# A fused attention and FFN kernel: attention blocks in another order on every engine, and the rows' turn one job later

## The chip, the cores and the metric

The kernel runs on one core of a Trainium2 chip. The metric is the time of one execution in device microseconds (us), and the median of several runs is compared.

## The reference

The input is one sequence of 2048 rows of 1024 numbers, in 32-bit floats. The reference is a block of a transformer with a norm before and after each half:

```python
x = x + _layernorm(attn(_layernorm(x), Wqkv, bqkv, Wo, bo))
x = x + _layernorm(ffn(_layernorm(x), W_gate, W_up, W_down))

# attn: one head of width 256
qkv = x @ Wqkv + bqkv                      # q, k, v: 2048 x 256 each
attn = softmax(q @ k.T / 16)               # 2048 x 2048
return (attn @ v) @ Wo + bo                # 2048 x 1024
# ffn, F = 2752
return (silu(x @ W_gate.T) * (x @ W_up.T)) @ W_down.T
```

## The kernel before, in words

**Precision.** A 32-bit product is made of three faster ones. Each operand is split into a high part (a copy by ScalarE, ACT, in a rounded format) and a low part (what is left, a subtraction by VectorE, DVE). `mm3` issues high times high, high times low and low times high. So every operand that reaches TensorE (PE) costs ACT one pass and DVE one pass.

**Stages.** First the queries, keys and values are made from the transposed input (to about 150 us). Then attention runs over 16 blocks of 128 queries, `i` from 0 to 15 (to about 400 us). Then comes the FFN in two halves of 1024 rows (`s` is 0 or 1), each with ten pairs of weight columns (`gate_up`) and a product with the down weights (`run_down`).

**One attention block.** While block `i` multiplies its probabilities with the values (`attend(i)`), the softmax of block `i+1` is prepared. In the ten blocks of `SPREAD` (2 to 11) the probabilities are turned with the help of DMAs:

- `scores(i+1, j)`, for four groups `j` of 512 keys: six matmuls and one reduce for the maximum on DVE (L266). `largest` joins the four (L465, L466).
- `exponentials(i+1, ...)`: four ACT passes into `p_s` (L476). After the second and the fourth, ACT's queue issues a store of one half to `pt_d` (L478), in pieces that go to other partitions.
- `collect(i)`: SP's queue loads the two halves of `pt_d` into `wr[0]` and `wr[1]` (L445). `turn_half` transposes each within 32 x 32 squares on DVE (L453), `high_half` (ACT, L457) and `low_half` (DVE, L461) split it.
- `turn_o(i-1)`: PE transposes the output of the block before (L524), ACT and DVE split it (L530, L531). `proj(i-1)` multiplies it with `Wo`, and DVE scales it and adds the bias (L541).
- `attend(i)`: 16 matmuls of 512 and 16 of 256 columns, in four quarters that need high half 0, low half 0, high half 1 and low half 1. ACT copies the sum (L516) and DVE adds the other part (L517).

**Queries.** The queries of the next four blocks come from `q_d` by `q_load` and are split by `q_split` (L435, L436). Blocks 4 to 7 use `qs[1]`, so its split must be done before block 3 computes the scores of block 4.

**Rows.** For the first `EARLY` = 8 blocks the rows that follow are done at once. `out_stats(t)` gives the norm of the projected row block (ACT, L555). `residual(t)` adds it to the row block of `x` (DVE, L559) and stores the sum in `x1_d` (L560). `rows_stats` (ACT, L566, and GpSimd, POOL) and `rows_norm` (ACT, L572) norm it. `spread(t)` stores it from ACT's queue to `xn_d` in another layout (L680), `gather(t)` loads it back on SP's queue (L683), `xpose(t)` transposes it on DVE (L687) and stores it in `xT_d` (L689), from where the FFN takes it. Each of these transfers moves 512 KB, as do the halves of `pt_d` and the load of `x` (L1295). Row blocks use three pairs of tiles in turn (`pair`), which lie in `f4` and `f2p`.

**Late rows.** Row blocks 8 to 15 store their projection in `at_d` (L543) and are finished during the ten pairs of the first FFN half. `gate_up` has four places where it takes one job from a list: after its first two products, after four, after eight and after ten. Before, the jobs of pair `p` are `between(p)` (the gather of the row block before), `ahead(p)` (its transpose, then the loads of the next, then `down_weights(p-1)`) and `behind(p)` (`load_down(p)`, then the norms of the next in `late_residual`, and its spread). The fourth place is used in the last pair alone.

**What sets the order.** The framework orders the instructions of each engine at compile time by a simulation. Instructions handed to `pin` (`tc.keep_in_program_order`) keep the order of the program among themselves on their engine. Engines and the queues that issue DMAs (SP's, ACT's) work in order, so an instruction that waits holds all that stand behind it. Before, the score matmuls and most of ACT's and DVE's work of a block are pinned, and the DMAs are not. Matmuls of a block are in this order: scores 0, 1 and 2, `turn_o`, scores 3, `proj`, `attend`.

Of the kernel before, what the change touches and what calls it, by code (L numbers as in the profile page):

```python
# [34 lines left out]
def block_kernel(ctx, tc, x, xt, wqk, wqk_t, wv, bqk, bv, wo, bo, wgu, wlast, wd, out):  # L35
# [390 lines left out]
    def o_of(i):  # L426

        return o_s[i % 2] if i < NT - 1 else xe[:, 0:D]
# [4 lines left out]
    def q_split(g, pin=lambda i: i):  # L433
        q = qs[g % 2]
        pin(nc.scalar.copy(q[:, :, 0, :], qraw))  # L435
        nc.vector.tensor_tensor(q[:, :, 1, :], qraw, f32(q[:, :, 0, :]), ALU.subtract)  # L436
# [6 lines left out]
    def collect(i):  # L443
        for h in range(2):
            nc.sync.dma_start(wr[h], pt_d[i][h])  # L445
# [53 lines left out]
    def attend(i, pin=lambda i: i):  # L499
# [3 lines left out]
        if i == NT - 1:  # L503
# [4 lines left out]
            nc.scalar.copy(o, b[:, :D])  # L508
# [7 lines left out]
        nc.scalar.copy(o, b[:, :D])  # L516
        nc.vector.tensor_tensor(o, b[:, D:], o, ALU.add)  # L517
# [16 lines left out]
    def proj(i, pin=lambda i: i):  # L534
# [7 lines left out]
        if i >= EARLY:  # L542
            nc.sync.dma_start(at_d[i], a)  # L543
# [14 lines left out]
    def residual(t, a, xt, r, pin):  # L558
        pin(nc.vector.scalar_tensor_tensor(xt, a, r, xt, ALU.mult, ALU.add))  # L559
        nc.sync.dma_start(x1_d[t].rearrange("(g s) c -> s g c", g=4), xt)  # L560
# [10 lines left out]
    def rows_norm(a, xt, r, m):  # L571
        nc.scalar.activation(a, xt, AF.Identity, bias=m, scale=r)  # L572
# [105 lines left out]
    def spread(t, a):  # L678

        nc.scalar.dma_start(by_quarter(xn_d[t]), a.rearrange("p (i c) -> p i c", i=4))  # L680

    def gather(t, b):
        nc.sync.dma_start(b, xn_d[t])  # L683

    def xpose(t, a, b):
# [3 lines left out]
        nc.sync.dma_start(d.rearrange("(j p) t -> p j t", p=P), a.rearrange("p (j t) -> p j t", j=8))  # L689
# [597 lines left out]
    sts = {}  # L1287
    for i in range(NT):
# [3 lines left out]
        if 4 <= i < EARLY + 4:  # L1292
            xpose(i - 4, *pair[(i - 4) % 3])
        if 4 <= i < EARLY + 1:
            nc.sync.dma_start(pair[(i - 1) % 3][1], x[(i - 1) * P : i * P, :])  # L1295
        if i == EARLY + 3:
            first_load(0, *room[0])
        if i in SPREAD:
            collect(i)
            scores(i + 1, 0, pin, pin)  # L1300
            scores(i + 1, 1, pin, pin)
            turn_half(i, 0)
            scores(i + 1, 2, pin, pin)
            turn_o(i - 1, pin, pin)
            high_half(i, 0)
            scores(i + 1, 3, pin, pin)
            largest(i + 1, pin)
            turn_half(i, 1)
            exponentials(i + 1, (0, 1), pin)
            high_half(i, 1)  # L1310
            exponentials(i + 1, (2, 3), pin)
            low_half(i, 0)
            proj(i - 1, pin)
            low_half(i, 1)
            denominator(i + 1, pin)
# [17 lines left out]

        if i < 2:
            wo_split(i)
        if i == 0:
            center_bo()
        if i == 1:
            q_load(1)
        if i == 2:  # L1340
            q_split(1, pin)
        if i % TB == 0 and TB <= i < NT - TB:
            q_split(i // TB + 1, pin)
        if 2 <= i < EARLY + 2:
            residual(i - 2, *pair[(i - 2) % 3], sts[i - 2], pin)
        if i < 3:
            nc.sync.dma_start(pair[i][1], x[i * P : (i + 1) * P, :])
        if i == NT - 1:
            for f in order[2:5]:
                f.use()  # L1350
            for f, r in zip(order[6:8], (wr[1], f4[1])):
                f.load(r)
        if i in SPREAD:
            attend(i, pin)
        else:
            if i > 0:
                turn_o(i - 1)
            attend(i)
            if i > 0:
                proj(i - 1)  # L1360
        if 2 <= i < EARLY + 2:
            of_rows = rows_stats(i - 2, *pair[(i - 2) % 3])
# [150 lines left out]
```

## Time and profile before

| What | Value |
|---|---|
| median of 3 runs (lowest, highest) | 1643.91 us (1643.29, 1647.49) |
| the profiled execution | 1645.07 us, of which the span of its instructions is 1643.3 us |
| PE busy | 1620.4 us, 99% of the span |
| DVE busy | 1117.9 us, 68% |
| ACT busy | 730.9 us, 44% |
| POOL busy | 113.5 us, 7% |
| data moved by DMA | 321.33 MB, 196 GB/s on the mean |
| matmul of 128x128 with 128x512 | 386 to 391 ns each, issued about every 0.23 us |

A busy time is the sum of an engine's instructions. Matmuls overlap (the next one is issued while one drains), so PE can be busy and still not issue at its full rate. A wait in the profile says who waited, and on whose instruction or transfer. The span is cut into stretches where a stage has its own limit: the ten spread blocks run from 176 to 331 us, the pairs of the first FFN half with late rows from about 550 to 800 us.

### The profile page before, as it was taken

How to read it: one execution, taken by the hardware profiler on the slowest of the kernel's cores; microseconds unless marked ns; L12 is line 12 of the kernel's file. 1: busy time of each engine (PE TensorE's matmuls, PEld its weight loads, DVE VectorE, ACT ScalarE, POOL GpSimd, SP SyncE). 2: the span in 40 equal slices, each digit the busy share in tenths (PEclk: the TensorE clock that was granted, in tenths of full speed). 3: DMA queues.
4: the chain of work that ended last, by engine and by line, in shares of the span. 5: the costliest groups of instructions: out<-in, count | busy, mean ns of one | idle time of the engine just before them, and what ended most of it. 6: DMA issues, size and time to landing. Idle time of an engine off the chain costs nothing.

```text
span 1643.3 us, 20534 instructions
## 1 busy us (share of the span) xinstructions
PE 1620.4 (99%) x7416; PEld 1343.8 (82%) x7416; DVE 1117.9 (68%) x1612; ACT 730.9 (44%) x1072; POOL 113.5 (7%) x176
## 2 busy tenths in 40 slices
PE   9999999999999999999999999999999999999998
PEld 8888777787888888888888888888888888888887
DVE  6656788778677777777577458855666655555458
ACT  5664565436444334443465344433333333354342
POOL 3120011000011111120000001100000000000001
PEclk9999999999999999999999999999999999999999
DMA  9451599856657777677477657632222233676653
GB/s 318 161 186 57 182 327 317 303 165 231 224 168 243 239 247 240 231 238 264 149 256 247 195 182 234 203 104 96 96 97 97 103 103 121 243 259 195 192 188 122
DMA packets 161622, 321.33 MB, mean 196 GB/s; under 512 B 15216, under 2 KB 50672, under 8 KB 161520
## 3 DMA queue, kind: packets, MB, share of 16 engines
q1 hardware_dynamic: 141360, 299.18, 54.7%
q10 hardware_dynamic: 20160, 20.84, 3.8%
q8 instruction: 58, 0.95, 0.2%
q14 instruction: 44, 0.36, 0.1%
HBM read 217.19 MB, written 102.78 MB: 195 GB/s over the span
## 4 chain that ended last, share of the span: by engine, by line
PE 75%; DMA 9%; DVE 9%; issue 3%; ACT 2%; POOL 2%; ACTq 0%; SPq 0%; DVEq 0%; POOLq 0%
PE bank L952 59%; DMA xn_d<-f 4%; PE bank L129 3%; PE bank L130 3%; PE bank L131 3%; DMA f<-xn_d 2%; DVE a L113 2%; PE bank L247 1%; PE bank L513 1%; PE bank L515 1%; ACT p_s L476 1%; POOL small L124 1%; DVE small L119 1%; PE bank L248 1%; DVE f L966 1%
## 5 line engine op out<-in xcount | busy, mean ns | idle before, releaser
L952 PE MATMUL bank<-a 128*128 128x512 f32 (+1 forms) x960 | 226.4, 386 | 0.0
L952 PE MATMUL bank<-xb,a 128*128 128x512 f32 x912 | 212.7, 389 | 0.1
L952 PEld LDWEIGHTS bank<-a 128*128 128x128 f32 x960 | 179.1, 188 | 36.5
L952 PEld LDWEIGHTS bank<-xb,a 128*128 128x128 f32 x912 | 170.8, 188 | 35.8 <-DVE a L113 0.5
L112 ACT CAST a<-f2p 128x1024 fp32r<-128x1024 f32 (+2 forms) x123 | 107.2, 871 | 140.6 <-PE bank L952 86.6
L113 DVE TENSOR_TENSOR a<-f2p,a 128x1024 fp32r<-128x1024 f32 (+2 forms) x123 | 122.5, 996 | 44.0 <-ACT a L112 37.0
L952 PE MATMUL bank<-kx,a 128*128 128x512 f32 x612 | 145.2, 389 | 0.0
L952 PEld LDWEIGHTS bank<-kx,a 128*128 128x128 f32 x612 | 114.9, 188 | 23.9
L113 DVE TENSOR_TENSOR a<-f,a 128x1024 fp32r<-128x1024 f32 (+1 forms) x70 | 80.0, 1143 | 64.0 <-ACT a L112 62.0
L952 PE MATMUL bank<-wvo 128*128 128x512 f32 (+1 forms) x498 | 120.9, 386 | 0.0
L952 PEld LDWEIGHTS bank<-wvo 128*128 128x128 f32 x498 | 93.0, 188 | 18.9
L952 PE MATMUL bank<-a,a 128*128 128x512 f32 x420 | 100.3, 391 | 2.5 <-ACT p_s L1014 1.2
L112 ACT CAST a<-f 128x1024 fp32r<-128x1024 f32 (+1 forms) x70 | 57.7, 824 | 98.7 <-PE bank L952 92.7
L952 PE MATMUL bank<-kx,wvo 128*128 128x512 f32 x420 | 99.3, 389 | 0.0
L952 PEld LDWEIGHTS bank<-a,a 128*128 128x128 f32 x420 | 78.4, 188 | 21.2 <-ACT p_s L1014 2.6
L952 PEld LDWEIGHTS bank<-kx,wvo 128*128 128x128 f32 x420 | 78.8, 188 | 16.4
L113 DVE TENSOR_TENSOR wvo<-f,wvo 128x1024 fp32r<-128x1024 f32 (+1 forms) x47 | 54.7, 1164 | 53.3 <-ACT wvo L112 53.3
L966 DVE TENSOR_TENSOR xi<-bank,xi 128x512 f32<-128x512 f32 (+1 forms) x90 | 60.9, 682 | 41.2 <-PE bank L952 34.7
L952 PE MATMUL bank<-a1b,wvo 128*128 128x512 f32 x360 | 86.8, 389 | 0.0
L966 DVE TENSOR_TENSOR p_s<-bank,p_s 128x512 f32<-128x512 f32 x80 | 53.9, 682 | 39.9 <-PE bank L952 36.0
L952 PEld LDWEIGHTS bank<-a1b,wvo 128*128 128x128 f32 x360 | 67.6, 188 | 14.0
L952 PE MATMUL bank<-kx 128*128 128x512 f32 (+1 forms) x339 | 78.5, 387 | 0.0
(366 smaller groups left out, 2982.4 us busy)
## 6 DMA issues: line engine op xcount, KB each, us to landing
f2p<-wgu SPq DMA_DIRECT2D x41, 512.0 KB, 5.5
f<-x SPq DMA_DIRECT2D x28, 512.0 KB, 5.8
f<-wgu SPq DMA_DIRECT2D x22, 512.0 KB, 3.5
wr<-wgu SPq DMA_DIRECT2D x21, 512.0 KB, 5.0
hd_S<-xi SPq DMA_DIRECT2D x42, 256.0 KB, 4.4
pt_d<-p_s ACTq DMA_DIRECT2D x20, 512.0 KB, 4.7
wr<-pt_d SPq DMA_DIRECT2D x20, 512.0 KB, 4.4
f<-wd SPq DMA_DIRECT2D x20, 512.0 KB, 4.3
```

The costliest lines, as they stand in the source:

```text
L112: nc.scalar.copy(hi, src)
L113: (lo_engine or nc.vector).tensor_tensor(lo, src, f32(hi), ALU.subtract)
L119: b = nc.vector.bn_stats(s[:, 6 * i : 6 * i + 6], h)
L124: nc.gpsimd.tensor_tensor(s[:, 15:16], s[:, 14:15], mhalf, ALU.pow)
L129: pin(nc.tensor.matmul(o, w[0], m[0], start=first, stop=False))
L130: pin(nc.tensor.matmul(o, w[0], m[1], start=False, stop=False))
L131: return pin(nc.tensor.matmul(o, w[1], m[0], start=False, stop=last))
L247: pin(nc.tensor.matmul(b, xg[:, c, 0, cols], wv_s[:, c, :, :].rearrange("p a f -> p (a f)"), start=(c == 0), stop=False))
L248: pin(nc.tensor.matmul(b[:, D:], xg[:, c, 1, cols], wv_s[:, c, 0, :], start=False, stop=(c == 7)))
L476: pin(nc.scalar.activation(o, b, AF.Exp, bias=s[:, 5:6], scale=1.0 / 16.0, accum_out=s[:, 8 + j : 9 + j]))
L952: one = nc.tensor.matmul(o, w[i], m[j], start=first and n == 0, stop=last and n == 2, skip_group_check=chained)
L966: nc.vector.tensor_tensor(o, a, b, op)
```

## The change

**The attention blocks.** A spread block is now a function of its own, `block(i)`, and all its instructions on all engines and queues are pinned. Against before:

- `turn_o(i-1)` stands behind the first scores instead of the third.
- The rows of block `i-2` are no longer done at the end of block `i` and on into the next. `rows_in` (residual and store) stands at the start of block `i`, `rows_squares` behind `turn_o`, `rows_out` (norm and spread) before the first high half. In block 2 alone the three stand at the end, before `out_stats`.
- At a block's end stand, in this order, `out_stats(i-1)`, the gather of row block `i-2`, the transpose and store of row block `i-3`, the load of `x`, the collect of the next block's first half, the denominator, the split of queries and `attend(i)`. The second half is collected at the next block's start.
- `q_split` does one half at a time, in two blocks (both halves in block 2).
- In block 9 the transpose of row block 6 writes to `xe` and not to its pair's tile, which is `f4[0]`.
- The output of the last block goes to the end of `p_s` instead of `xe`, and its copy is pinned before the splits of three FFN operands.

**The late rows.** `xpose` of the row block before and the loads of the next move from `ahead` to `behind`. `late_residual` and `spread` move from `behind` to a fourth job, `rows`.

```diff
     def o_of(i):
-        return o_s[i % 2] if i < NT - 1 else xe[:, 0:D]
+        return o_s[i % 2] if i < NT - 1 else p_s[:, T - D :]
...
-    def q_split(g, pin=lambda i: i):
+    def q_split(g, d):
         q = qs[g % 2]
-        pin(nc.scalar.copy(q[:, :, 0, :], qraw))
-        nc.vector.tensor_tensor(q[:, :, 1, :], qraw, f32(q[:, :, 0, :]), ALU.subtract)
+        pin(nc.scalar.copy(q[:, d, 0, :], qraw[:, d]))
+        pin(nc.vector.tensor_tensor(q[:, d, 1, :], qraw[:, d], f32(q[:, d, 0, :]), ALU.subtract))
...
-    def collect(i):
-        for h in range(2):
-            nc.sync.dma_start(wr[h], pt_d[i][h])
+    def collect(i, h):
+        pin(nc.sync.dma_start(wr[h], pt_d[i][h]))
...
+    def load_x(t):
+        pin(nc.sync.dma_start(pair[t % 3][1], x[t * P : (t + 1) * P, :]))
+
+    def rows_in(t):
+        if 0 <= t < EARLY:
+            residual(t, *pair[t % 3], sts[t], pin)
+
+    def rows_squares(t):
+        if 0 <= t < EARLY:
+            of_rows[t] = rows_stats(t, *pair[t % 3])
+
+    def rows_out(t):
+        if 0 <= t < EARLY:
+            rows_norm(*pair[t % 3], *of_rows[t])
+            spread(t, pair[t % 3][0], pin)
+
+    def block(i):
+        first = i == SPREAD[0]
+        if not first:
+            rows_in(i - 2)
+        collect(i, 1)
+        scores(i + 1, 0, pin, pin)
+        turn_o(i - 1, pin, pin)
+        if not first:
+            rows_squares(i - 2)
+        scores(i + 1, 1, pin, pin)
+        scores(i + 1, 2, pin, pin)
+        turn_half(i, 0)
+        if not first:
+            rows_out(i - 2)
+        high_half(i, 0)
+        scores(i + 1, 3, pin, pin)
+        largest(i + 1, pin)
+        turn_half(i, 1)
+        exponentials(i + 1, (0, 1), pin)
+        high_half(i, 1)
+        exponentials(i + 1, (2, 3), pin)
+        low_half(i, 0)
+        proj(i - 1, pin)
+        low_half(i, 1)
+        if first:
+            rows_in(i - 2)
+            rows_squares(i - 2)
+            rows_out(i - 2)
+        if i - 1 < EARLY:
+            sts[i - 1] = out_stats(i - 1, pair[(i - 1) % 3][0])
+        if i - 2 < EARLY:
+            gather(i - 2, pair[(i - 2) % 3][1], pin)
+        if 0 <= i - 3 < EARLY:
+            a, b = pair[(i - 3) % 3]
+            xpose(i - 3, xe if i - 1 == EARLY else a, b, pin)
+            if i < EARLY:
+                load_x(i)
+        if i + 1 in SPREAD:
+            collect(i + 1, 0)
+        denominator(i + 1, pin)
+        if i == 2:
+            q_split(1, 0)
+            q_split(1, 1)
+        elif i % TB < 2:
+            q_split(i // TB + 1, i % TB)
+        attend(i, pin)
...
     def ahead(p):
...
-        if late(p - 1):
-            a, b = rooms(p - 1)
-            xpose(late(p - 1), a, b)
-        if late(p):
-            a, b = rooms(p)
-            nc.sync.dma_start(a, at_d[late(p)])
-            nc.sync.dma_start(b, x[late(p) * P : (late(p) + 1) * P, :])
         down_weights(p - 1)
...
             load_down(p)
+        if late(p - 1):
+            xpose(late(p - 1), *rooms(p - 1))
+        if late(p):
+            a, b = rooms(p)
+            nc.sync.dma_start(a, at_d[late(p)])
+            nc.sync.dma_start(b, x[late(p) * P : (late(p) + 1) * P, :])
+
+    def rows(p):
         if late(p):
             a, b = rooms(p)
             late_residual(late(p), a, b)
...
-            jobs = [] if s else [lambda: between(p), lambda: ahead(p), lambda: behind(p)]
+            jobs = [] if s else [lambda: between(p), lambda: ahead(p), lambda: behind(p), lambda: rows(p)]
             if s == 0 and p == NPAIR - 1:
-                jobs.append(lambda: down_weights(NPAIR - 1))
+                jobs[-1] = lambda: down_weights(NPAIR - 1)
```

The stores and loads of the other row functions (`residual`, `spread`, `gather`, `proj`) and the copies of `attend` get a `pin` of their own.

## The prediction

> **What bounds the kernel now.** I read the page, busy time stretch by stretch, the waits of PE, then the timelines of the queues in the attention blocks.
>
> ```profile
> PE 1620.4 (99%) x7416; PEld 1343.8 (82%) x7416; DVE 1117.9 (68%) x1612; ACT 730.9 (44%) x1072; POOL 113.5 (7%) x176
> DMA  9451599856657777677477657632222233676653
> ```
>
> TensorE (PE) sets the end nearly everywhere; where the DMA digits stand at 9 (the sixth and seventh slices, 205 to 288 us) lie the attention blocks.
>
> ```profile
> 190.16:204.75 14.59, 14.30 (x72) 11.76 (x71) 12.01 (x18) 9.07 (x17) 1.87 (x6) 1.00 0.86 293
> 204.75:218.94 14.19, 14.19 (x72) 11.77 (x71) 12.19 (x19) 10.03 (x18) 1.88 (x6) 1.00 0.95 315
> 249.37:265.37 16.00, 14.32 (x72) 11.77 (x71) 11.93 (x18) 9.07 (x17) 1.68 (x5) 1.00 0.99 330
> 295.66:314.51 18.85, 15.93 (x72) 12.90 (x71) 11.21 (x18) 8.04 (x15) 0.93 (x3) 0.91 0.89 307
> ```
>
> Blocks 3, 4, 7 and 10 (length, busy PE, PEld, DVE, ACT, POOL, clock, DMA share): the same 72 matmuls take 14.19 to 18.85 us. Blocks 2 to 10 last 138.5 us (176.0 to 314.51); nine of 14.05 would be 126.5. So 12.0 us are there to win, 1.7 of it a clock of 0.91 over 18.85 us after a PE idle of 2.9 us.
>
> ```profile
> PE bank L129 <- DVE oTs L531: 6.2, 6, 2.9
> PE bank L524 <- ACT xe L508: 2.5, 1, 2.5
> PE bank L515 <- DVE a L461: 1.8, 2, 1.4
> ```
>
> PE waits for output's transposes (L531), for the last block's output (L508), and for the low half (L461). Behind these stand transfers:
>
> ```profile
> 223.98 7.47 DMA xT_d<-f
> 231.55 1.41 DVE f L541 x2
> ...
> 265.34 4.11 DMA wr<-pt_d
> 269.48 1.25 DVE wr L453
> ...
> 293.46 6.39 DMA at_d<-f
> 299.94 1.25 DVE f L687
> ```
>
> The chain: a row's transposed store holds the projection's L541, the collect of turned probabilities holds L453, the store of `at_d` holds the row transpose L687.
>
> ```profile
> 222.87 0.32 SPq L445 DMA_DIRECT2D wr<-pt_d  x1
> 223.28 0.65 SPq L560 DMA_DIRECT2D x_d<-f2p  x1
> 223.98 0.58 SPq L689 DMA_DIRECT2D xT_d<-f  x1
> 224.62 1.50 SPq L1295 DMA_DIRECT2D f<-x  x1
> ```
>
> SP's queue now: the collects go ahead of the row's store and x load. Landings come one after another: the third of these lands at 231.45 (above), with ACT's `xn_d` store issued between, so the last of four lands 8.58 us after the first issue; a collect alone takes 4.11: (8.58-4.11)/3 = 1.49 us for each further 512 KB. A row block moves nine of them, 13.4 us of a 14.05 us block.
>
> **Part 1, transposes of output behind the first scores.** They move from 6 matmuls before the projection to 18 (12 x 0.2275 = 2.7 us earlier). They need the block before's output: its ACT copy and DVE add end about 1.05 us into the block, the first six scores issue until 1.37. So 0 where DVE is free. The 6.2 us of waits go unless something else holds the blocks.
>
> **Part 2, rows.** Row work runs at a block's start, its transpose at the end. So L541 no longer meets the store (2.7 us of DVE idle), and row 6's transpose writes `xe`, away from `at_d`'s store (3.25 us). But SP's pinned order is now: gather, xT store (needs the transpose, last on DVE), x load, and only then the next block's first collect. This closes a loop. Its DVE part, from a block without waits:
>
> ```profile
> 318.07 1.23 DVE L453 STREAM_TRANSPOSE wr<-wr 128x1024 f32<-128x1024 f32 x1
> ...
> 326.13 0.15 DVE L482 TENSOR_REDUCE ys<-ys 128x1 f32<-128x4 f32 x1
> ```
>
> 8.06 us from the first turn to the end of the low halves; less one reduce (0.60), L531 (0.34) and a wait (0.23), which now come before it, plus the row transpose 1.25: 8.14. The second collect queues behind the first and the x1 store, so it lands 2 x 1.49 = 2.98 later, while DVE asks for it 2.1 later: +0.9. Then SP (0.1), then xT store, load and collect: the store alone 4.2 (the shortest of `xT_d`), two more 2.98: 7.2. The loop is 8.14+0.9+0.1+7.2 = 16.3 us, over PE's 14.05. Without the x load (from block 8 on) it is 14.8. Blocks 4 to 10 follow five loops of 16.3 and two of 14.8 = 111.1; the last queries' load gets between once, +1.5; before they took 314.51-204.75 = 109.8. So +2.8 in place of the gain; block 11 +0.4. Bounds: 14.05 for all seven, -11.4; with 1 us more queueing a block, +10.
>
> The Trainium skill (DMA: Bandwidth & Descriptors, Anatomy of one DMA) fits another issue path with 2.0 us plus bytes/436 GB/s, 1.2 us for 512 KB. By it three transfers take 5.6 us and the loops 14.7 and 14.05; the blocks would lose 8 us of their 109.8. The rows above have 1.49 and 4.1 to 4.2, so I keep those.
>
> **Part 3, the first block.** In block 2, row 0's work and out_stats(1) come before the split of the next queries (L435) on ACT, and block 3's first scores need that split.
>
> ```profile
> 187.76 1.05 ACT L435 CAST qb<-f 128x1024 fp32r<-128x1024 f32 x1 [0.46 <-ACT p_s L476]
> 191.30 1.16 ACT L566 ACTIVATE f<-f,small 128x1024 f32<-128x1024 f32 x1 [0.57 <-DVE f L559]
> 193.76 1.25 ACT L572 ACTIVATE f<-f,small 128x1024 f32<-128x1024 f32 x1 [0.17 <-POOL small L568]
> 195.03 0.37 ACTq L680 DMA_DIRECT2D xn_d<-f  x1
> ```
>
> Now the split runs at 187.76, before. After: low halves end at 187.6, L559 1.28, L566 at 188.9, L572 2.46 later at 191.4, the issue until 193.0, out_stats 1.14, the halves of the split at 194.2 and 194.7, DVE until 196.1. PE wanted it at 190.16: it idles 4.7 us at first and a little within. Gather 0 goes out at 196.5 (row 0's store issued 192.6, 3.9 to land), block 3's first collect behind it lands 4.2+1.49 later, 202.2; PE ends that block 9.1 after (two turns, reduce, largest, the wait of 0.9 and the first low half 5.3, then attend's last three quarters 3.7): 211.4 against 204.75, +6.6. Bounds: +4.7 (the idle alone) and +8.3 with a clock loss of 1.7 as in block 10.
>
> The Trainium skill (TensorE: Matmul & The Clock Gate, What's actually happening) halves the clock after some 3.4 us of idling, by a free-running window; the trace has it after 2.9 us and not after 2.5 (L524). By either, this pause slows PE for a while. Block 3 waits for its collect anyway, so I add nothing.
>
> **Part 4, rows' turn one job later in the first FFN half.**
>
> ```profile
> 603.68 1.25 DVE L687 STREAM_TRANSPOSE f<-f 128x1024 f32<-128x1024 f32 x1 [7.36 <-DMA f<-xn_d]
> ```
>
> DVE stands 7.4 us a pair at L687 for the gather, and PE loses little: 2.5 us idle in 560 to 800 in six gaps, and each restart costs 0.16 more (a matmul lasts 0.39 us, the next one issues 0.23 after it): 3.5. With the transpose one job (24 matmuls, 5.5 us) later and the statistics too, DVE should reach L687 when the gather has landed: -3.3. Moved past on SP: two loads, one store, one gather that waits for its store (5 us of SP). If a weight load is late behind it, it costs instead: bounds -3.5 and +4 (half a us a pair, as PE loses now).
>
> **Part 5, the end.** Output of the last block goes to `p_s`, so L508 (2.5 us of PE idle at 399.2) needn't wait for L747. But the split of `qb` ends at 402.3 on DVE and the next matmuls need it: 0 (bounds -2.6 and +1). Splitting q in halves: 0.1 a time, hidden on ACT (44% busy).
>
> **Sum.** +6.6 +2.8 +0.4 -3.3 = +6.5. The profiled execution took 1645.07 us (span 1643.3 and 1.8 around it), 1.2 above the median of 1643.91; I add to the median: 1650.4.
>
> **Rivals.** (a) Faster: transfers keep up. Decides: if the last of the three lands within 14.05-9.14 = 4.9 us of the store's issue, PE sets blocks 4 to 10: -11.4, the pause in block 2 alone +4.9, FFN -3.3: -9.8, 1634.1. For it: the shortest landing on `pt_d` is 3.0 us; against: DMA shares of 0.95 to 0.99. (b) Between: store 4.2 and 1.3 a transfer, no second wait: loops 15.0 and 14.05, 103.1 us, -6.7; +6.1 for block 2, -3.3: -3.9, 1640.0. (c) As forecast, but SP's gather holds FFN's weights: +4 in place of -3.3: 1657.7.
>
> **Numbers.** Forecast 0.53, (a) 0.15, (b) 0.20, (c) 0.12. What a measurement can tell from no change is 0.3%, 4.9 us: under 1639.0 and over 1648.8. Of the forecast 0.45 lies over, 0.08 within; (b) 0.15 within, 0.05 under; (a) under; (c) over. Faster 0.20, same 0.23, slower 0.57. Range 1640 to 1659: it leaves out (a) and the far end.
>
> **What would show it.** After: PE idle of 4 to 5 us at the start of block 3 for `qb` (L435/436), with a clock under 1; L453 waiting for `wr<-pt_d` in most blocks and blocks near 16 us; L531 gone from PE's waits; L687 no longer waiting 7 us in the FFN. Wrong, if blocks 4 to 8 take 14.1 us, or if no idle stands before block 3.

## The result, and the profile after

The changed kernel took 1658.05 us (median of 4 runs, 1657.28 to 1658.41), the kernel before 1645.54 us beside it (4 runs, 1643.29 to 1647.49). The ratio is 1.0076, with a 95% interval of 1.0058 to 1.0093: slower, as forecast, by about twice the size forecast (+12.5 us against +6.5) and some 1 us inside the upper end of the range. The profiled execution has a span of 1655.5 us, 12.2 more than before.

Line numbers of the changed kernel are one below those of before nearly everywhere (L452 is the turn that was L453, L456 and L460 the high and the low half, L951 the FFN's L952); the split of the queries keeps L435 and L436, and the `x` load is L1289. In e4 and e8 the numbers are those of before. The page:

```profile
PE 1624.5 (98%) x7416; PEld 1348.3 (81%) x7416; DVE 1115.6 (67%) x1615; ACT 733.1 (44%) x1075; POOL 101.0 (6%) x176
DMA  8451588865647877777477656633222233676563
```

The sixth and seventh slices of DMA have fallen from 9 to 8: the same bytes take longer. The first waits of PE (total, times, longest), and the first of DVE between 190 and 345 us:

```profile
PE bank L514 <- DVE a L460: 7.0, 6, 1.9
PE bank L512 <- ACT a L456: 6.4, 5, 2.2
PE bank L129 <- ACT qb L435: 5.0, 1, 5.0
PE bank L951 <- ACT qb L745: 1.7, 1, 1.7
PE bank L951 <- DVE qb L746: 1.3, 1, 1.3
```

```profile
DVE wr L452 <- DMA wr<-pt_d: 23.9, 15, 3.3
```

The waits for output's transposes (6.2 us) are gone. In their place PE waits 13.4 us for the halves of the turned probabilities, because DVE now waits 23.9 us for the collects (3.9 before). Blocks 3, 4, 5, 7 and 10 (length, busy PE, PEld, DVE, ACT, POOL, clock, DMA share, GB/s):

```profile
194.97:213.00 18.03, 16.45 (x70) 13.38 (x71) 13.49 (x20) 9.43 (x18) 2.26 (x7) 0.87 0.79 269
213.00:229.26 16.26, 14.57 (x72) 11.70 (x71) 12.29 (x19) 9.69 (x18) 1.69 (x6) 1.00 0.89 282
229.26:247.28 18.02, 15.85 (x72) 12.94 (x71) 13.36 (x20) 9.69 (x18) 2.12 (x7) 0.91 0.87 270
265.99:281.16 15.17, 14.27 (x73) 11.78 (x72) 12.13 (x18) 9.18 (x17) 1.67 (x5) 1.00 0.85 295
313.41:329.05 15.64, 14.56 (x73) 11.70 (x71) 11.59 (x18) 5.54 (x12) 0.00 (x0) 1.00 0.77 267
```

None takes the 14.05 us that its matmuls need. To see where each stretch wins or loses, I compared the start of the same matmul (by its number in the order of PE) in two traces. For the changed kernel, in us behind the kernel before: 8.25 at the start of block 4, 14.54 at the start of block 11, 14.71 at the last block, 16.80 at the FFN's beginning (440 us), 12.53 at 800 us, 12.21 at the end. This comparison is called the ledger below, where every experiment has it too.

How block 2 ends shows on ACT's timeline:

```profile
189.12 1.15 ACT L565 ACTIVATE f<-f,small 128x1024 f32<-128x1024 f32 x1 [1.63 <-DVE f L558]
...
191.57 1.24 ACT L571 ACTIVATE f<-f,small 128x1024 f32<-128x1024 f32 x1 [1.21 <-POOL small L567]
...
193.26 1.06 ACT L554 ACTIVATE xe<-f 128x1024 f32<-128x1024 f32 x1 [0.44 <-ACT f L571]
...
194.31 1.12 ACT L435 CAST qb<-f 128x512 fp32r<-128x512 f32 x2
```

Squares and norm of row 0 and the squares of row 1 stand ahead of the split, which starts at 194.31 (187.76 before). PE stands idle from 189.98 to 194.97. And SP's queue in a later block (start, time):

```profile
228.99 0.37 SPq L688 DMA_DIRECT2D xT_d<-f  x1
229.41 0.57 SPq L1289 DMA_DIRECT2D f<-x  x1
230.07 1.09 SPq L444 DMA_DIRECT2D wr<-pt_d  x1
231.51 0.53 SPq L559 DMA_DIRECT2D x_d<-f  x1
232.14 0.54 SPq L444 DMA_DIRECT2D wr<-pt_d  x1
```

The half that the first collect loads had landed in `pt_d` at 228.89, but the collect goes out behind the row's store and the `x` load, and lands at 237.64. DVE's turns show the loop that this makes:

```profile
202.34 1.23 DVE L452 STREAM_TRANSPOSE wr<-wr 128x1024 f32<-128x1024 f32 x1
206.76 1.25 DVE L452 STREAM_TRANSPOSE wr<-wr 128x1024 f32<-128x1024 f32 x1 [2.23 <-DMA wr<-pt_d]
220.44 1.25 DVE L452 STREAM_TRANSPOSE wr<-wr 128x1024 f32<-128x1024 f32 x1 [2.18 <-DMA wr<-pt_d]
...
237.66 1.25 DVE L452 STREAM_TRANSPOSE wr<-wr 128x1024 f32<-128x1024 f32 x1 [3.15 <-DMA wr<-pt_d]
...
288.72 1.25 DVE L452 STREAM_TRANSPOSE wr<-wr 128x1024 f32<-128x1024 f32 x1 [2.31 <-DMA wr<-pt_d]
```

From the first turn of block 3 to that of block 8 there are five loops in 288.72 - 202.34 = 86.4 us, 17.3 each; 18.1 and 17.2 are the first two.

### The profile page after: what moved, and what is told of

Read it like the earlier page. It is cut to its first block, busy times and chain, and to the rows that moved or that the text cites. A ratio compares the mean times of both kernels' runs of the same rounds, so it can differ in the third digit from the quotient of the medians.

```text
span 1655.5 us, 20573 instructions
## 1 busy us (share of the span) xinstructions
PE 1624.5 (98%) x7416; PEld 1348.3 (81%) x7416; DVE 1115.6 (67%) x1615; ACT 733.1 (44%) x1075; POOL 101.0 (6%) x176
## 4 chain that ended last, share of the span: by engine, by line
PE 89%; DMA 4%; DVE 3%; ACT 2%; issue 1%; SPq 0%; POOL 0%; ACTq 0%; POOLq 0%; DVEq 0%
PE bank L951 73%; DMA wr<-pt_d 3%; PE bank L130 3%; PE bank L131 3%; PE bank L129 3%; PE bank L512 2%; PE bank L247 1%; PE bank L514 1%; PE bank L248 1%; PE bank L494 1%; DVE a L460 1%; ACT p_s L475 1%; PE bank L312 1%; DVE wr L452 1%; PE bank L1138 0%
## 5 line engine op out<-in xcount | busy, mean ns | idle before, releaser
L951 PE MATMUL bank<-a 128*128 128x512 f32 (+1 forms) x960 | 226.4, 386 | 0.0
L951 PE MATMUL bank<-xb,a 128*128 128x512 f32 x912 | 212.4, 389 | 0.0
L951 PEld LDWEIGHTS bank<-a 128*128 128x128 f32 x960 | 179.1, 188 | 36.5
L951 PEld LDWEIGHTS bank<-xb,a 128*128 128x128 f32 x912 | 170.9, 188 | 35.5 <-DVE a L113 0.2
L951 PE MATMUL bank<-kx,a 128*128 128x512 f32 x612 | 145.2, 389 | 0.0
L951 PEld LDWEIGHTS bank<-kx,a 128*128 128x128 f32 x612 | 114.9, 188 | 23.8
L113 DVE TENSOR_TENSOR a<-f,a 128x1024 fp32r<-128x1024 f32 (+1 forms) x70 | 66.9, 956 | 95.3 <-ACT a L112 93.2
L951 PE MATMUL bank<-wvo 128*128 128x512 f32 (+1 forms) x498 | 120.9, 386 | 0.0
L951 PEld LDWEIGHTS bank<-wvo 128*128 128x128 f32 x498 | 93.0, 188 | 18.9
L951 PE MATMUL bank<-a,a 128*128 128x512 f32 x420 | 99.4, 389 | 0.0
L951 PE MATMUL bank<-kx,wvo 128*128 128x512 f32 x420 | 99.3, 389 | 0.0
L951 PEld LDWEIGHTS bank<-a,a 128*128 128x128 f32 x420 | 78.8, 188 | 16.4
L951 PEld LDWEIGHTS bank<-kx,wvo 128*128 128x128 f32 x420 | 78.8, 188 | 16.4
L951 PE MATMUL bank<-a1b,wvo 128*128 128x512 f32 x360 | 86.6, 389 | 0.0
L951 PEld LDWEIGHTS bank<-a1b,wvo 128*128 128x128 f32 x360 | 67.6, 188 | 14.0
L951 PE MATMUL bank<-kx 128*128 128x512 f32 (+1 forms) x339 | 78.5, 387 | 0.0
```

The source lines that it names most:

```text
L113: (lo_engine or nc.vector).tensor_tensor(lo, src, f32(hi), ALU.subtract)
L951: one = nc.tensor.matmul(o, w[i], m[j], start=first and n == 0, stop=last and n == 2, skip_group_check=chained)
```

## Experiments

The ledger of all runs, each from one profile: us behind (+) or ahead of (-) the kernel before at the same matmul.

| Kernel | block 4 | block 11 | last block | 440 us | 800 us | end | blocks 4 to 10 take |
|---|---|---|---|---|---|---|---|
| before | 0 | 0 | 0 | 0 | 0 | 0 | 109.76 |
| changed | +8.25 | +14.54 | +14.71 | +16.80 | +12.53 | +12.21 | 116.05 |
| e1 split first | +9.53 | +15.71 | +15.89 | +19.22 | +14.95 | +14.83 | 115.94 |
| e2 first collect first | +5.65 | +8.52 | +11.87 | +12.70 | +8.42 | +8.00 | 112.63 |
| e3 e1 and e2 | +8.57 | +10.99 | +16.98 | +18.09 | +13.82 | +13.40 | 112.17 |
| e4 FFN part only | -0.03 | +2.85 | +2.85 | +2.29 | -1.99 | -1.34 | 112.64 |
| e5 both collects first | +6.20 | +0.72 | +0.55 | +4.01 | -0.27 | -0.09 | 104.28 |
| e6 e5, block 2 as before | +7.49 | +0.24 | +0.07 | +0.77 | -3.51 | -3.70 | 102.51 |
| e7 e6, casts first | +7.12 | +1.10 | +0.93 | +1.92 | -2.36 | -2.43 | 103.75 |
| e8 turn_o only | +1.86 | +9.91 | +9.75 | +9.30 | +9.67 | +9.25 | 117.81 |
| e9 e5, row 0 early | +1.86 | -2.22 | -2.39 | -0.30 | -4.57 | -4.95 | 105.67 |
| e10 e6, statistics first | +2.74 | -3.74 | -3.91 | -1.95 | -6.22 | -5.17 | 103.28 |
| e11 e9, casts first | +1.36 | -5.52 | -5.70 | -5.97 | -10.24 | -10.56 | 102.88 |

One profile of the attention blocks is good to some 3 us only: e4 has the same code there as the kernel before and took 112.64 us for 109.76, e9 and e11 are alike there and took 105.67 and 102.88. The profiled execution of e2 is the shortest of its five, 3 us under their median; that of e11 lies 2 us under its median, that of e8 2.5 over. Ratios below come from the repeated runs against the kernel before.

**e1: the split ahead of row 0's work** (on the changed kernel).

```diff
         if first:
+            q_split(1, 0)
+            q_split(1, 1)
             rows_in(i - 2)
             rows_squares(i - 2)
             rows_out(i - 2)
...
-        if i == 2:
-            q_split(1, 0)
-            q_split(1, 1)
-        elif i % TB < 2:
+        if i != 2 and i % TB < 2:
```

> The changed kernel, with the split of the next queries (L435, L436) ahead of row 0's work in block 2. Theory (SP's order sets block 3, not ACT's): PE's idle of 5.0 us before block 3 goes, but block 3's first collect still stands behind row 0's gather on SP, so PE idles inside block 3 instead; block 4 begins at 211 to 213 us (213.0 in the changed kernel), and the time falls by 0 to 2 us, to 1656 to 1658. Rival (the queue of ACT is the whole price of part 3): block 4 begins at 205 to 208 us, and the time falls by 5 to 8 us, to 1650 to 1653.

It took 1659.31 us, ratio 1.0097 (1.0079 to 1.0115): no gain. Block 3 begins at 190.29, and PE then idles inside it:

```profile
PE bank L523 <- DVE f L516: 5.8, 1, 5.8
```

What waits now is output's transposes: its copy (L515) runs at 196.77 on ACT, behind the squares and the norm of row 0 and the squares of row 1. Block 4 begins at 214.28, later than the 211 to 213 expected. So the theory holds in its core, that the idle moves, but not in its detail: the wait that takes over is on ACT, before SP's collect comes into it.

**e2: the first collect ahead on SP.**

```diff
+        if i + 1 in SPREAD:
+            collect(i + 1, 0)
         if i - 2 < EARLY:
             gather(i - 2, pair[(i - 2) % 3][1], pin)
         if 0 <= i - 3 < EARLY:
             a, b = pair[(i - 3) % 3]
             xpose(i - 3, xe if i - 1 == EARLY else a, b, pin)
             if i < EARLY:
                 load_x(i)
-        if i + 1 in SPREAD:
-            collect(i + 1, 0)
```

> The changed kernel, with the next block's first collect put on SP ahead of the gather, the row transpose's store and the x load; nothing else moved. Theory (the loop through SP): DVE's waits for the collect (23.9 us in 190 to 345 us) fall under 6; blocks 4 to 10 take 14.1 to 15.2 us each, 99 to 106 us together (116.05 in the changed kernel); the idle of 5.0 us before block 3 stays, block 4 begins at 208 to 210.5; the time falls by 13 to 20 us, to 1638 to 1645. Rival 1 (the 512 KB transfers fill the DMA engines, whatever their order): another transfer is late in the collect's place, blocks 4 to 10 stay over 110 us together, and the time falls by less than 6. Rival 2 (the new order on DVE and ACT is what costs): nothing changes, 1656 to 1659.

1656.17 us, ratio 1.0083 (1.0066 to 1.0101). The theory fell short: blocks 4 to 10 took 112.63 us, not 99 to 106. (Block 4 began at 210.40, as expected.) DVE still waits 19.2 us for `wr<-pt_d`, in 8 waits of up to 5.0, and all of them now stand at the second turn of a block; the first turn waits nowhere. In block 3 the first collect landed at 194.17, 6.7 us earlier than in the changed kernel, and yet the first turn starts only 0.8 us earlier (202.34 there):

```profile
201.57 1.23 DVE L452 STREAM_TRANSPOSE wr<-wr 128x1024 f32<-128x1024 f32 x1
```

So in block 3 it isn't the first collect that the turn stands for. Why the second turns wait shows on SP's queue about the start of block 5:

```profile
222.40 0.32 SPq L444 DMA_DIRECT2D wr<-pt_d  x1
222.82 0.37 SPq L682 DMA_DIRECT2D f2p<-xn_d  x1
225.67 0.37 SPq L688 DMA_DIRECT2D xT_d<-f  x1
226.09 1.40 SPq L1289 DMA_DIRECT2D f<-x  x1
228.20 0.53 SPq L559 DMA_DIRECT2D x_d<-f  x1
```

The second half's store is issued by ACT at 223.39, behind the first collect and the gather, and lands only at 229.81 (6.42 us); the second collect goes out at 229.87, behind three more transfers, and lands at 236.03 (6.15). Transfers of the rows have slipped in ahead of each step of the second half. This is the rival of another transfer that is late in the collect's place.

**e3: e1 and e2 together.**

> The changed kernel with both edits: the split ahead of row 0's work, and the first collect ahead on SP. Theory: with the collect no longer behind row 0's gather, the idle of 5.0 us before block 3 goes and comes back nowhere; block 4 begins at 204 to 206 us, and the time is 4 to 6.5 us under that of the collect's move alone, 1633 to 1640. Rival (row 0's work on ACT and DVE is late in any case, and holds block 3 by its low halves): block 4 begins at 208 us or later, and the time is within 2 us of the collect's move alone.

1656.44 us, ratio 1.0083 (1.0066 to 1.0101): nothing over e2. Block 4 begins at 213.32, and the 5.8 us for L523 stand as in e1. The rival was right: row 0's work at the end of block 2 costs some 5 us of PE whoever stands in front of it.

**e4: the FFN part alone, on the kernel before.** 

```diff
 def ahead(p):
...
-        if late(p - 1):
-            xpose(...)
-        if late(p):
-            ...                # the loads from at_d and x
         down_weights(p - 1)
 def behind(p):
...
             load_down(p)
+        if late(p - 1):
+            xpose(...)
+        if late(p):
+            ...                # the loads from at_d and x
+def rows(p):
         if late(p):
             a, b = rooms(p)
             late_residual(late(p), a, b)
             spread(late(p), a)
...
-jobs = [..., lambda: behind(p)]
+jobs = [..., lambda: behind(p), lambda: rows(p)]
```

> The kernel before, with only the rows' turn of the first FFN half moved one job later (part 4). Theory: DVE's waits at the row transpose (7.4 us a pair) go, PE's idles of 2.5 us in 560 to 800 us and their restarts go, and the time falls by 3.3 to 4.2 us, to 1641 to 1642. Rival 1: the weight loads stand behind the moved transfers on SP, and the time rises by 0.5 to 4 us. Rival 2: the gain seen there in the changed kernel comes from elsewhere (what attention left in the queues), and the time stays within 1 us.

1641.44 us, ratio 0.9991 (0.9978 to 1.0005). The ledger falls from +2.29 to -1.99 between 440 and 800 us: -4.28, and -4.27 in the changed kernel. In both, PE is busy for all of 560 to 800 us (240.00; 237.54 before). Before, DVE waited there

```profile
DVE f L687 <- DMA f<-xn_d: 36.5, 5, 7.6
```

and neither kernel with the new turn shows that wait. So part 4 is worth 4.3 us in this stretch, by two traces. For the whole kernel the repeated runs show less: 1.5 us, with an interval from a gain of 3.6 us to a loss of 0.8. The profile of e4 loses 2.85 us in the attention blocks, where its instructions stand in the order of before on every engine; whether that is more than the spread of single profiles isn't shown.

**e5: both collects ahead, right behind the gather.**

```diff
-        collect(i, 1)
...
+        if i + 1 in SPREAD:
+            collect(i + 1, 0)
+            collect(i + 1, 1)
         if 0 <= i - 3 < EARLY:
             a, b = pair[(i - 3) % 3]
             xpose(i - 3, xe if i - 1 == EARLY else a, b, pin)
             if i < EARLY:
                 load_x(i)
-        if i + 1 in SPREAD:
-            collect(i + 1, 0)
```

> The changed kernel, with both collects of the next block on SP right behind the gather and ahead of the row transpose's store, the x load and the row's store: SP's order of before, with the change's order on all other engines. What the two runs with one collect moved left open: the first collect was early there, and DVE waited for the second one. Theory (SP's order alone lengthens blocks 4 to 10): DVE's waits for both collects fall from 23.9 us (190 to 345 us) to under 8, PE's idles in blocks 4 to 10 to under 3 us together, and these blocks take 100 to 106 us (116.05 in the changed kernel, 109.8 before); block 3 still begins 5 us late behind the split, and block 4 begins 6 to 8.3 us later than before; the time is 1639 to 1648. Rival (the transfers' bytes are the bound: nine of 512 KB at 1.5 us each are 13.4 of 14.05 us): the row's stores and loads come late in their place, L560's and L689's tiles hold DVE, blocks 4 to 10 stay over 110 us, and the time stays over 1651.

1644.77 us, ratio 1.0000 (0.9988 to 1.0012): the 12 us of the change are back, by SP's order alone. Blocks 4 to 10 took 104.28 us, and DVE's waits are

```profile
DVE wr L452 <- DMA wr<-pt_d: 6.4, 7, 2.1
```

SP's queue at the start of block 5:

```profile
225.52 1.69 SPq L444 DMA_DIRECT2D wr<-pt_d  x2
227.30 0.39 SPq L688 DMA_DIRECT2D xT_d<-f  x1
227.74 0.57 SPq L1289 DMA_DIRECT2D f<-x  x1
228.36 0.56 SPq L559 DMA_DIRECT2D x_d<-f  x1
```

The second collect waits on SP for its half to land in `pt_d` (226.82), and the row's three transfers go out only behind it. The collects land at 231.15 and 232.51, 5.6 us after issue each; the row's three land 6.8 to 8.8 us after theirs, and no wait of DVE names them. Block 3 still began 5 us late, behind the split, as expected. The rival of the bytes is out: the same nine transfers fit into 14.9 us on the mean (104.28 / 7).

**e6: block 2 in the order of before as well.** 

```diff
         if first:
-            rows_in(i - 2)
-            rows_squares(i - 2)
-            rows_out(i - 2)
-        if i - 1 < EARLY:
+            q_split(1, 0)
+            q_split(1, 1)
+        if not first and i - 1 < EARLY:
             sts[i - 1] = out_stats(i - 1, pair[(i - 1) % 3][0])
-        if i - 2 < EARLY:
+        if not first and i - 2 < EARLY:
             gather(i - 2, pair[(i - 2) % 3][1], pin)
...
         attend(i, pin)
+        if first:
+            rows_in(i - 2)
+            rows_squares(i - 2)
+            rows_out(i - 2)
+            sts[i - 1] = out_stats(i - 1, pair[(i - 1) % 3][0])
+            gather(i - 2, pair[(i - 2) % 3][1], pin)
```

> The kernel with both collects ahead, and block 2's order of before too: the split of the next queries, then attend, then row 0's work, out_stats(1) and row 0's gather. Theory: the idle of 5 us before block 3 goes and comes back nowhere; block 4 begins within 1 us of the kernel before (204.75 us); the time is 6 to 8 us under that of both collects alone, 1632 to 1641, faster than before by 0.2 to 0.7%. Rival (row 0's work is only pushed into block 3 and holds DVE and ACT there): block 4 begins 3 us late or more, and the time is within 4 us of both collects alone.

1643.35 us, ratio 0.9994 (0.9985 to 1.0004). The rival was right; block 4 begins 7.49 us late. Waits of PE, then of DVE:

```profile
PE bank L129 <- DVE oTs L530: 4.9, 1, 4.9
```

```profile
DVE f L558 <- POOL small L548: 6.3, 1, 6.3
```

The residual of row 1 (L558) is now the first instruction of block 3 on DVE. It needs the statistic of `out_stats(1)`, which stands on ACT behind row 0's squares and norm, and L530 stands behind it. The kernel before could afford this order in block 2, since it asked for row 1's residual a whole block later.

**e7: the casts of the next weights ahead of attend's copy at the last block** (on e6).

```diff
+            if i == NT - 1:
+                for f in order[2:5]:
+                    f.use()
+                for f, r in zip(order[6:8], (wr[1], f4[1])):
+                    f.load(r)
             attend(i)
-            if i == NT - 1:
-                ...            # the same
```

> The same (both collects ahead, block 2's order of before), and at the last block the casts of the next weights (L745, L746) ahead of attend's copy on ACT and DVE, as before the change; the output stays in the other tile. Theory: the 1.69 and 1.33 us that PE waits for these casts at 414 to 418 us in the changed kernel go, no wait of 2.5 us for output's copy comes back since the copy has its own tile, and the stretch from the last block to the FFN is 2 to 4 us shorter than in the changed kernel (where it is 2.1 longer than before). Rival: ACT and DVE do the casts late in any order, since their data land late; the waits stay, and the stretch is within 1 us of the changed kernel.

1641.28 us, ratio 0.9980 (0.9970 to 0.9990). On ACT in the changed kernel, and in e7:

```profile
412.56 0.37 ACT L507 COPY p_s<-bank 128x256 f32<-128x256 f32 x1 [3.80 <-PE bank L506]
412.83 1.05 ACT L745 CAST kx<-wr 128x1024 fp32r<-128x1024 f32 x1
```

```profile
397.51 1.05 ACT L745 CAST kx<-wr 128x1024 fp32r<-128x1024 f32 x1 [2.53 <-DMA wr<-xs_d]
...
400.52 0.36 ACT L507 COPY p_s<-bank 128x256 f32<-128x256 f32 x1
```

In the changed kernel ACT stands 3.80 us for the last attend, with the casts behind it. In e7 it casts meanwhile, and PE's idles there fall from 1.69 and 1.33 us to 0.81 and 1.13. The theory was half right: 1.1 us less idle, and a wait of 0.81 for the copy, which I had said would not come. From the last block to 440 us this stretch is 1.1 us shorter than in the changed kernel, where 2 to 4 were expected; but e6, with the casts late, is 1.4 shorter too, since its clock stayed full there (below). By the medians the casts' place is worth 2.1 us (e6 to e7) and 2.6 us (e9 to e11), but in both pairs the intervals overlap.

**e8: `turn_o` behind the first scores, on the kernel before, and nothing else.**

```diff
             scores(i + 1, 0, pin, pin)
+            turn_o(i - 1, pin, pin)
             scores(i + 1, 1, pin, pin)
             turn_half(i, 0)
             scores(i + 1, 2, pin, pin)
-            turn_o(i - 1, pin, pin)
```

> The kernel before, with output's transposes behind the first scores and nothing else changed (part 1 alone). Theory (the blocks are held by the transfers and DVE, output's transposes only showed it): PE's 6.2 us of waits for L531 go, waits for the low halves or the turned probabilities come in their place, blocks 2 to 10 take 136 to 140 us (138.5 before), and the time stays within 2 us of before. Rival 1 (the wait was the loss): blocks 2 to 10 take 130 to 134 us, and the time falls by 4 to 8 us. Rival 2 (output's copy and low half now stand ahead of the first turn on DVE, and push it): the blocks take over 141 us.

1651.86 us, ratio 1.0040 (1.0022 to 1.0058): slower. Blocks 2 to 10 took 147.55 us (138.5 before), as the second rival has it. In block 4 on ACT:

```profile
207.08 1.16 ACT L566 ACTIVATE f<-f,small 128x1024 f32<-128x1024 f32 x1
...
208.22 1.05 ACT L555 ACTIVATE xe<-f2p 128x1024 f32<-128x1024 f32 x1
...
209.54 1.24 ACT L572 ACTIVATE f<-f,small 128x1024 f32<-128x1024 f32 x1 [0.18 <-POOL small L568]
...
211.22 0.38 ACT L530 CAST oTs<-bank 128x256 fp32r<-128x256 f32 x1 [0.44 <-PE bank L131]
```

With the rows' work still at a block's end, it runs on ACT in the first 4 us of the next block, just where output's copy would be. DVE waits for that copy 17.5 us in 7 waits, with the first turn behind it, and PE 11.6 us for low halves (1.8 before). So the move of `turn_o` needs the move of the rows' work; the latter alone was not tried.

**e9: row 0 spread over block 2, both collects ahead, the split first.** The special case of block 2 is taken out, on top of e5 and of e1's split.

```diff
-        if not first:
-            rows_in(i - 2)
+        rows_in(i - 2)
...
-        if not first:
-            rows_squares(i - 2)
+        rows_squares(i - 2)
...
-        if not first:
-            rows_out(i - 2)
+        rows_out(i - 2)
...
         if first:
             q_split(1, 0)
             q_split(1, 1)
-            rows_in(i - 2)
-            rows_squares(i - 2)
-            rows_out(i - 2)
```

> Both collects ahead, the split of the next queries ahead of out_stats(1), and row 0's work not at block 2's end but spread over block 2 as every later row's is over its block (residual first, squares behind output's transposes, norm behind the first turn). What the run with block 2's order of before left open: PE's 5 us had only moved, to L530 at 196.5 us, because the residual of row 1 at block 3's start (L558) waited 6.3 us for a statistic that stood on ACT behind row 0's squares and norm. Theory (it is these 3.6 us of row 0 on ACT, at a block's end, that cost; anywhere else they are hidden): row 0's residual waits for its own statistic until about 179 us and holds block 2's first turn by 1 us, then no idle over 1 us stands in block 3; block 4 begins 0.5 to 2 us later than before (7.5 with block 2's order of before); the time is 1635 to 1640, a ratio of 0.994 to 0.997. Rival (the first blocks have no room for two rows' work whatever its place): 4 us or more of idle come back in block 2 or 3, block 4 begins at least 5 us late, ratio 0.998 or more.

1639.15 us, ratio 0.9964 (0.9952 to 0.9976). Block 4 begins 1.86 us late, with one idle of 1.30 us in block 2. The theory holds.

**e10: e6 with `out_stats(1)` ahead of attend.**

```diff
-        if not first and i - 1 < EARLY:
+        if i - 1 < EARLY:
             sts[i - 1] = out_stats(i - 1, pair[(i - 1) % 3][0])
...
             rows_out(i - 2)
-            sts[i - 1] = out_stats(i - 1, pair[(i - 1) % 3][0])
             gather(i - 2, pair[(i - 2) % 3][1], pin)
```

> Both collects ahead; block 2's end in the order split, out_stats(1), attend, and only then row 0's work and gather: the run with block 2's order of before, with out_stats(1) alone moved ahead. Theory: L558 in block 3 finds its statistic and waits under 1 us (6.3 there), but row 0's squares and norm (2.4 us of ACT) still stand ahead of output's copy (L529) in block 3, so L530 holds PE by 1 to 3 us in place of 4.9; block 4 begins 2 to 5 us later than before; the time is 1637 to 1642. Rival (L558's wait was not what held PE): the idle of 4.9 us at L530 stays, and block 4 begins 7 us late.

1638.96 us, ratio 0.9966 (0.9955 to 0.9978). The wait of 6.3 us at L558 is no longer among DVE's, PE waits 1.4 us for L530 in place of 4.9, and block 4 begins 2.74 us late. So it was L558's statistic that held PE in e6.

**e11: e9 with e7's casts.**

> Row 0's work spread over block 2, both collects ahead, and the casts of the next weights ahead of attend's copy at the last block: the best of all runs put together. Theory: the stretch from the last block to the FFN is 0 to 2 us shorter than without the casts' move, and the attention blocks are as there; the time is 1633 to 1639, a ratio of 0.993 to 0.997 to the kernel before. Rival: the casts' place is worth nothing, and the two agree within 1 us.

1636.58 us, ratio 0.9953 (0.9941 to 0.9966): 0.5% faster than the kernel before, and 1.2% than the changed one (0.9953 / 1.0076 = 0.988). Its blocks 4 and 10:

```profile
206.11:220.11 14.00, 14.00 (x72) 11.85 (x71) 12.31 (x19) 9.69 (x18) 2.39 (x8) 1.00 0.90 296
...
292.78:308.99 16.21, 14.54 (x72) 11.69 (x71) 11.68 (x18) 5.54 (x12) 0.00 (x0) 1.00 0.86 303
```

The first has PE's own length, with the clock at 1.00. Some 3 us are still lost in blocks 4 to 10 (102.88 less seven times 14.05 and 1.5 for the queries' load).

## Why the prediction was right, and where it was short

The direction, the places, the loop through SP and the gain in the FFN were right; the path through block 3, three sizes and the end were not. The errors of the terms add up to 5.7 of the 12.2 us, and the time stayed inside the range by some 1 us. It lies next to the 1657.7 of rival (c), whose mechanism didn't come, so the number alone would have named the wrong cause. The terms, by the ledger (each from one profile, so good to some 3 us in the attention blocks):

- **Part 3, the start of block 4: +6.6 forecast, +8.25 measured.** The idle was 4.98 us (4.7), row 0's gather went out at 195.84 (196.5), the first collect landed at 200.86 (202.2). But the sum went through that collect, and block 3 didn't: its first turn (202.34, above, with no wait) followed the third scores (their reduce starts at 201.74), which PE had late after its pause and at half clock, and e2, where the collect landed before block 3 began, has the turn 0.8 us earlier only. So "Block 3 waits for its collect anyway, so I add nothing" was wrong: the pause and the clock (0.87 over the block) were the path. That the forecast 202.2 is close to 202.34 is luck. After that the second turn waited 2.23 us for the second collect (206.76, above), where I had put 0.9; in e5 that wait is gone and the pause stays, and block 4 begins 6.20 us late. e1 doesn't decide this, since its pause only moved (5.8 us for L523).
- **Part 2, blocks 4 to 10: +2.8 forecast, +6.3 measured** (+3.3 if e1 is set against e4, which have the order of the changed kernel and of before in these blocks). The loop was there, 17.3 us for the 16.3 of the sum. From the row's store to the first collect's landing it took 7.7, 8.7, 7.8, 6.8 and 7.8 us, 7.75 on the mean, for my 7.2; the second turn waited 1.29 us on the mean of the five (2.23, 0.36, 0.53, 1.79, 1.55) for my 0.9. The row's store alone was even quicker than I had it (3.55 to 3.78 us in the five, not 4.2), but the `x` load landed 1.7 to 3.6 us after it, and not 1.49, and the collect 1.3 to 2.0 us after that. The 1.49 was read a little low: it set 4.11 us of another collect against the four transfers, while the first of the four itself landed after 3.59 (226.46), which gives (8.58 - 3.59) / 3 = 1.66 us each, and 7.5 for the three. What the sum did not see is that the second collect has a loop of its own: e2 took the first one out of its loop and gained 3.4 us at most in these blocks (by its one profile; its ratio shows none of it), both together 11.8 (116.05 to 104.28). The fit of the Trainium skill that the prediction weighed (DMA: Bandwidth & Descriptors, Anatomy of one DMA), made for another issue path, gives an estimate of 5.6 us for the three transfers; with 7.75 measured, the 7.2 from the rows was the better guide, and still too low.
- **Part 4, FFN: -3.3 forecast, -4.3 measured** twice (changed kernel and e4). Mechanism right, the size 1 us small, and outside the bound of -3.5. Rival (c), the weight loads held by the gather, didn't come.
- **Part 5, the end: 0 forecast, +2.1 measured**, outside its bounds. The step that failed took the split of `qb` as fixed in time. It isn't: output's copy was pinned ahead of the casts on ACT, and so the casts waited for the last matmul of attend (3.80 us). PE's idle grew by 0.5 us (1.69 + 1.33 for 2.49), and the other 1.6 are about what one stretch of half clock takes (1.7, below).
- **Part 1, 0 by itself**: right in the changed kernel, where L530's waits went and others came. Alone it loses 0.4%, 6.6 us (e8): I had not asked what stands on ACT ahead of the copy when the rows' work isn't moved too.
- **Rival (a), transfers that keep up,** was a matter of order: with both collects ahead of the row's transfers (e5, e6, e7 and e9 to e11) blocks 4 to 10 take 102.5 to 105.7 us. The rival had 98.4. (The sum of rival (b) left out the queries' load, for which the forecast added 1.5.)

Sum: 8.25 + 6.29 + 0.17 (block 11 to the last) + 2.09 - 4.27 - 0.32 (the tail) = 12.21.

Still open: the part of the `x` load by itself was not tried, nor row 6's transpose into `xe` (DVE's wait of 3.2 us for `at_d` is gone in the changed kernel); and the 3 us by which profiles of the same attention code differ have no cause shown here.

## What to carry to other kernels

On a queue that works in order, put the transfers that the next block waits for ahead of those that have a block's time, all of them: one early and its twin behind the bulk gains little (e2 against e5). By the rows of e5, the early one's wait for its data may also serve as a gate that keeps the bulk back; that was not tried by itself. When work moves to where the next block starts, look at its first use and at what stands ahead of it on every engine there, for the first block apart, since a special case at the start (row 0 here) can cost as much as the steady order. And compare matmul by matmul, stretch by stretch: the sum of this change hid +6.3, -4.3, +8.3 and +2.1 us.

## What the runs showed of the hardware

**The same idles cost a clock loss or none, by where they fall.** At the last block PE idles 1.69 us, works for 1.0, and idles 1.33 or 1.34 us, alike in the changed kernel, in e5 and in e6. Over the 12 us from the start of these idles the mean clock is 0.86, 0.72 and 1.00. The records of the granted clock in the traces say more: it changes only at points that lie whole windows of 3.41 us apart. Here are such windows (columns as above, clock third from the end), for the changed kernel, e5 and e6:

```profile
414.60:418.02 3.42, 1.01 (x3) 0.48 (x3) 3.42 (x4) 3.42 (x6) 0.00 (x0) 1.00 0.73 244
418.02:421.43 3.41, 3.27 (x8) 2.59 (x9) 3.41 (x7) 2.54 (x6) 0.00 (x0) 0.50 0.80 260
```

```profile
399.95:403.36 3.41, 1.03 (x4) 0.48 (x3) 3.41 (x4) 3.41 (x6) 0.00 (x0) 1.00 0.78 288
403.36:406.78 3.42, 2.77 (x7) 2.20 (x8) 3.42 (x6) 2.05 (x4) 0.00 (x0) 0.50 0.83 253
406.78:410.19 3.41, 3.41 (x10) 2.64 (x9) 3.00 (x5) 1.88 (x4) 0.00 (x0) 0.50 0.82 289
```

```profile
397.72:401.14 3.42, 1.77 (x10) 1.22 (x8) 1.83 (x3) 3.22 (x5) 0.00 (x0) 1.00 0.63 244
401.14:404.55 3.41, 2.03 (x7) 1.34 (x8) 3.41 (x6) 2.85 (x5) 0.00 (x0) 1.00 0.79 279
```

In the changed kernel and in e5 most of the idle falls into one window (2.4 us without PE), and the next is at half clock. In e6 it is split over two (1.65 and 1.38 us), and no clock is lost. Each window at half clock costs 1.7 us of work: one in the changed kernel, two in e5, where the first of them still held 0.64 us of idle. All thirteen traces agree: of some 6200 windows at full clock, the 35 with 1.84 us or more without PE were followed by half clock, and none with 1.79 or less was (of two between, at 1.80 and 1.81 us, one was). After a window at half clock, 0.64 us or more of idle in it kept the clock low, and 0.36 us or less brought it back. A single idle of 2.17 us (237.87 to 240.04, in the changed kernel's block 5) lay in one window and cost the clock of the next. So the 2.9 us that cost a clock before the change had 2.65 in one window, while the 2.49 us at the last block were 1.61 and 0.88 in two. Where the windows lie differs from run to run, so a sum made ahead can give such a loss only as a range, but a single idle under 1.8 us cost none by itself. The Trainium skill (TensorE: Matmul & The Clock Gate, What's actually happening) has a window of some 3.4 us that runs freely, and half clock after one idle window. The window is in these traces; but it need not be all idle, since 1.8 of its 3.41 us were enough here.

**Issued earlier, landed earlier, across two queues.** In e2 the second half's store goes out on ACT's queue behind the first collect and the gather on SP's, and takes 6.42 us to land; its collect goes out behind the row's three transfers and takes 6.15. In e5 the store goes out ahead of the gather and both collects and takes 4.14, and its collect, ahead of the row's three, 5.6. Of the 153 pairs of transfers, one on SP's queue and one on ACT's, that were in flight together between 175 and 345 us in e2 and e5, the one issued first landed first in 148. So a transfer that is needed soon can be late behind others of another queue. That the collect waiting on SP (226.82, e5) is what keeps the row's transfers from getting ahead fits these rows; it was not tried by itself.
